# Attention in cycles of two pairs of heads, with their score blocks next to each other

## The chip, the cores and the metric

One core of one Trainium2 chip runs the kernel. The metric is the device time of one execution in microseconds (us). The core has five engines that each work through an instruction queue of their own: TensorE (PE, matrix products into the eight PSUM banks), VectorE (DVE), ScalarE (ACT), GpSimd (POOL) and SyncE (SP, which here issues nearly all DMA transfers).

## The reference

The input x has 32 sequences of 64 tokens of width 512. The context has the same shape. There are 32 heads of width 128.

```python
def reference(x, ctx, bias, mask, g_xattn, g_ffn, Wq, Wk, Wv, Wo, W, b, A, B, starts):
    q = layernorm(x) @ Wq                      # (32, 64, 32, 128)
    k, v = ctx @ Wk, ctx @ Wv
    score = einsum('bqhd,bkhd->bhqk', q, k) / sqrt(128) + bias
    probs = softmax(where(mask, score, -inf))  # masked entries are 0
    att = einsum('bhqk,bkhd->bqhd', probs, v) @ Wo
    x = x + tanh(g_xattn) * att
    n = layernorm(x)
    y = n @ W.T + b + where(use_lora, (n @ A.T) @ B.T, 0)   # adapter by sequence
    return x + tanh(g_ffn) * y
```

## The kernel before

The tokens are worked in two phases of 1,024 (`NPH`); a phase has eight tiles of 128 tokens (`NT`) and 16 pairs of heads (`NPR`). Nearly every large product is made of two parts per operand, a rounded high part and the rest, with three matmuls for each term (`mm3`). The projections q, k and v are also split into 2 x 2 blocks, and seven block products named p1 to p7 replace eight; `unit` computes them into the four banks px, py, pv and pz in the order p1, p6, p7, p5, p2, p4, p3, of which p2, p4 and p3 accumulate into px, pv and pz again, after these have been read once. ACT copies px into the destination, DVE adds the others to it. Each product is six matmuls of 128 x 128 weights by 512 columns.

A phase has three stages. `stage_a` computes all keys (stored to HBM as `kd`) and all values (`vd`). `run` is the attention: for each pair n of heads the q unit (42 matmuls into `qT`), `scores` (for each of two heads 16 products that fill halves of one bank, of 128 x 64 weights), the softmax, `pv` (probabilities by values into four banks, copied and split into `ch` and `cl`), and `oproj` (eight token tiles of six matmuls with the split output weights of the pair, added into `acc`). After the second phase's attention come the four chunks of the feed-forward part (`ffn_chunk`).

The order of work is written out by hand: every engine takes its instructions in the order in which the program issues them, and a matmul that needs a buffer waits for it there. Work off the matmuls is spread by generators that stand in the list `streams`. `beat()`, called after each product and each tile, takes one step of each of them, and `drain(g)` takes all that are left of one. Among them are `prep` (the blocks of the next q weights: seven casts on ACT, eleven operations on POOL), `prep_o` (the split of the output weights), `bias_mask` (mask added to the loaded bias, on POOL) and `softmax`. The scores of a head are worked on where they are issued:

```python
nc.vector.scalar_tensor_tensor(s, ps, SCALE, s, ALU.mult, ALU.add)     # L761, frees the bank
nc.vector.tensor_reduce(mx, s, AX.X, ALU.max)                          # L763
nc.gpsimd.tensor_tensor(s, s, mx.unsqueeze(2).to_broadcast([P, NT, S]), ALU.subtract)  # L764
nc.scalar.activation(s, s, AF.Exp)                                     # L765
beat()
```

The rest of the softmax goes by beats: sum, reciprocal, product with the row mask (L780 to L782, DVE), normalisation (L783, POOL), two 32 x 32 block transposes into `tp` (L775, DVE) and sixteen copies of a quarter into the block-diagonal tile `pt` (L792, ACT). Pair 0 of a phase has half of its copies done as transposes on DVE.

The cycle of pair n is: q unit up to p2, two oproj tiles of pair n - 2, the unit's p4 and p3, pv(n - 1), scores of n, six oproj tiles of pair n - 1. Scores are followed by oproj, but for pair 0, which has the next q unit behind it. PSUM tiles come from one pool of eight banks in turn. One buffer holds the pair's keys (`res[1]`, loaded after the scores of the pair before), two hold the values of two pairs, half of the tokens each (`res[2]`, `res[3]`), two hold `qT`, one `pt`, two the scores (`sm`), two `tp`.

Of the kernel before, what the change touches and what calls it, by code (L numbers as in the profile page):

```python
# [17 lines left out]
P = 128  # L18
# [3 lines left out]
S = 64  # L22
# [20 lines left out]
def flamingo_block(ctx: ExitStack, tc: tile.TileContext, x, ctxT, bias, mask, gx, gf,  # L43
# [24 lines left out]
    def drain(g):  # L68
        if g in streams:
            streams.remove(g)  # L70
            for _ in g:
                pass
# [625 lines left out]
    def attention(p, res, rest):  # L698
        b = {}

        def load_k(n):
            b["k", n] = big(res[1], [P, 2, TP], F32, f"kB{p}_{n}")
            nc.sync.dma_start(out=b["k", n], in_=kd[p][n])

        def load_v(q):
            b["v", q] = [big(res[2 + c], [P, 4, 512], F32, f"v{p}_{q}_{c}") for c in range(2)]
            for c in range(2):
                nc.sync.dma_start(out=b["v", q][c], in_=vd[p][q][:, c * 4:(c + 1) * 4, :])
# [5 lines left out]
        def bias_mask(n):  # L714
            yield
            yield
            for i in range(2):
                yield
                t = sm[n % 2][:, i]
                nc.gpsimd.tensor_tensor(t, t, masks[p][0], ALU.add)  # L720

# [5 lines left out]
        def enter():  # L727
# [10 lines left out]
            load_k(0)  # L738
            load_v(0)
# [28 lines left out]
        def softmax(n, pace):  # L768
            ss = [sm[n % 2][:, i] for i in range(2)]
            alone = pace is None  # L770
            tp = []

            def turn(i):
                tp.append(rows.tile([P, NT, S], F32, tag="row", name=f"tp{p}_{n}_{i}"))
                nc.vector.transpose(tp[i].rearrange("p a b -> p (a b)"), ss[i].rearrange("p a b -> p (a b)"))  # L775

            for i in range(2):
                nm = f"{p}_{n}_{i}"
                r = st.tile([P, NT], F32, tag="r", name=f"r{nm}")
                nc.vector.tensor_reduce(r, ss[i], AX.X, ALU.add)  # L780
                nc.vector.reciprocal(r, r)
                nc.vector.tensor_tensor(r, r, masks[p][1], ALU.mult)  # L782
                nc.gpsimd.tensor_tensor(ss[i], ss[i], r.unsqueeze(2).to_broadcast([P, NT, S]), ALU.mult)  # L783
                if alone and i:
                    turn(0)
                yield
            quads = [(h, qi, ki) for h in range(2) for qi in range(2) for ki in range(2)]

            def copy(f, i, of, h, qi, ki):
                src = slice(h * 64 + qi * 32, h * 64 + qi * 32 + 32)  # L790
                dst = slice(h * 64 + ki * 32, h * 64 + ki * 32 + 32)
                f(pt[dst, i, :, src], of[src, :, ki * 32:(ki + 1) * 32])  # L792

            if alone:
                for k, q in enumerate(quads):
# [361 lines left out]
```

## Time and profile before

| | us |
|---|---|
| median of 3 runs (1547.86 to 1548.68) | 1547.89 |
| the profiled execution | 1547.98 |
| its span, first to last instruction | 1545.8 |
| PE busy | 1538.4 |
| POOL busy | 1015.8 |
| DVE busy | 946.5 |
| ACT busy | 728.6 |

The granted TensorE clock is 1.000 over the span. The profile's page lists busy times, costliest groups by line and the chain of work that ended last; the chain of waits, the timeline and windows of it are answers from the same trace. The attention of the two phases runs from about 327 to 745 us and from 1060 to 1490 us. A busy PE is a modelled figure: records of matmuls overlap, and the starts of successive ones tell its pace. PE's L96 is the line of `mm3`, so its groups are told apart by tile (pa is oproj; px, py, pv, pz with q are the q unit; po is pv; ps is scores; ppk the plain key product). L87 and L88 are `split`, L293 and L297 the casts and differences of the weight blocks, L352, L357 and L374 the adds and copies of `unit`, L820 and L821 those of pv, L841 that of oproj.

### The profile page before, as it was taken

To read this page: it belongs to the slowest core of one execution; us is meant where nothing else is said; L and a number is where in the kernel's file an instruction comes from. 1 tells how busy PE (TensorE), PEld (TensorE's weight loads), DVE (VectorE), ACT (ScalarE), POOL (GpSimd) and SP (SyncE) were. 2 spreads that over 40 slices of the span, in tenths; PEclk is the share of its full clock that TensorE was granted. 3 is DMA by queue.
4 is the path that set the end of the run, shared out by engine and by line. 5 is a ranking of instruction groups with operands and counts; after the bars stand their busy time and mean duration, and the time that the engine had idled before them with its cause. 6 is when DMAs were issued, how large, how long until landed. Compare 5 with 4: busy or idle time off the path is not lost.

```text
span 1545.8 us, 24999 instructions
## 1 busy us (share of the span) xinstructions
PE 1538.4 (100%) x9080; PEld 1295.4 (84%) x9080; DVE 946.5 (61%) x1579; ACT 728.6 (47%) x1605; POOL 1015.8 (66%) x1128
## 2 busy tenths in 40 slices
PE   9999999999999999999999999999999999999999
PEld 7888888888888888888888888888888888888887
DVE  5675343377676757575686536437666676757763
ACT  6354233345555555556435423334555555555620
POOL 3898378967665757575589837896666665757410
PEclk9999999999999999999999999999999999999999
DMA  6654444374243424441565544438424342544201
GB/s 211 239 191 177 167 169 163 137 280 177 83 177 137 167 85 176 187 150 65 215 213 191 177 170 165 164 136 290 167 85 176 137 175 84 179 182 161 68 35 67
DMA packets 80989, 246.37 MB, mean 159 GB/s; under 512 B 9857, under 2 KB 10881, under 8 KB 72674
## 3 DMA queue, kind: packets, MB, share of 16 engines
q1 hardware_dynamic: 80578, 244.26, 43.9%
q8 instruction: 71, 1.16, 0.3%
q10 hardware_dynamic: 288, 0.52, 0.1%
q14 instruction: 52, 0.43, 0.1%
HBM read 171.35 MB, written 73.40 MB: 158 GB/s over the span
## 4 chain that ended last, share of the span: by engine, by line
PE 96%; DMA 2%; DVE 2%; issue 0%; ACT 0%; POOL 0%; SPq 0%; DVEq 0%; ACTq 0%; POOLq 0%
PE pa L96 22%; PE po L817 7%; PE pzv L96 6%; PE pvv L96 6%; PE pxv L96 6%; PE pzq L96 5%; PE pxq L96 5%; PE pxk L96 5%; PE pzk L96 5%; PE pvk L96 5%; PE pvq L96 5%; PE ps L759 4%; PE pf L96 4%; PE ppk L96 3%; PE pyv L96 3%; PE pyk L96 2%
## 5 line engine op out<-in xcount | busy, mean ns | idle before, releaser
L96 PE MATMUL pa<-wo,ch 128*128 128x512 f32 x1024 | 319.9, 393 | 0.0
L792 ACT COPY pt<-tp 32x256 f32<-32x256 f32 x496 | 200.3, 404 | 87.3 <-DVE tp L775 76.2
L88 POOL TENSOR_TENSOR wo<-rawo,wo 128x512 fp32r<-128x512 f32 x64 | 81.2, 1288 | 223.1 <-ACT wo L87 215.3
L96 PEld LDWEIGHTS pa<-wo,ch 128*128 128x128 f32 x1024 | 189.4, 188 | 40.0
L841 DVE TENSOR_TENSOR acc<-pa,acc 128x512 f32<-128x512 f32 x256 | 170.0, 673 | 79.5 <-PE pa L96 79.3
L96 PE MATMUL pa<-wo,cl 128*128 128x512 f32 x512 | 199.7, 390 | 0.0
L817 PEld LDWEIGHTS po<-pt,v 128*128 128x128 f32 x1024 | 119.1, 192 | 2.6 <-ACT pt L792 0.2
L821 DVE TENSOR_TENSOR cl<-po,ch 128x512 fp32r<-128x512 f32 x128 | 88.3, 691 | 51.9 <-ACT ch L820 51.4
L817 PE MATMUL po<-pt,v 128*128 128x128 f32 x1024 | 119.4, 275 | 0.0
L352 DVE TENSOR_TENSOR vt<-pvv,vt 128x512 f32<-128x512 f32 x64 | 44.1, 689 | 113.3 <-PE pvv L96 113.3
L96 PEld LDWEIGHTS pa<-wo,cl 128*128 128x128 f32 x512 | 96.1, 188 | 20.7
L820 ACT CAST ch<-po 128x512 fp32r<-128x512 f32 x128 | 75.0, 586 | 72.0 <-PE po L817 71.4
L765 ACT ACTIVATE sm<-sm 128x512 f32<-128x512 f32 x64 | 40.5, 633 | 122.7 <-POOL sm L764 122.7
L764 POOL TENSOR_TENSOR sm<-sm,mx 128x512 f32<-128x512 f32 x64 | 66.9, 1048 | 45.6 <-DVE mx L763 45.6
L374 ACT COPY vt<-pxv 128x512 f32<-128x512 f32 x32 | 18.8, 588 | 132.7 <-PE pxv L96 132.7
L352 DVE TENSOR_TENSOR kT<-pvk,kT 128x512 f32<-128x512 f32 x56 | 38.5, 688 | 69.4 <-PE pvk L96 68.8
L720 POOL TENSOR_TENSOR sm<-sm,madd 128x512 f32<-128x512 f32 x60 | 76.4, 1296 | 2.7 <-DMA sm<-bias 2.7
L783 POOL TENSOR_TENSOR sm<-sm,r 128x512 f32<-128x512 f32 x64 | 66.9, 1045 | 14.5 <-DVE r L782 11.1
L759 PE MATMUL ps<-kB,qT 128*64 128x64 f32 x2048 | 67.2, 224 | 0.3 <-DVE qT L352 0.3
L352 DVE TENSOR_TENSOR qT<-pzq,qT 128x512 f32<-128x512 f32 x64 | 44.2, 691 | 38.0 <-PE pzq L96 37.6
L352 DVE TENSOR_TENSOR vt<-pzv,vt 128x512 f32<-128x512 f32 x64 | 44.2, 691 | 37.1 <-PE pzv L96 36.9
L759 PEld LDWEIGHTS ps<-kB,qT 128*64 128x64 f32 x2048 | 62.5, 138 | 4.9 <-issue 0.7
(976 smaller groups left out, 3706.2 us busy)
## 6 DMA issues: line engine op xcount, KB each, us to landing
kd<-kT SPq DMA_DIRECT2D x64, 512.0 KB, 3.2
vd<-vt SPq DMA_DIRECT2D x128, 256.0 KB, 2.3
kB<-kd SPq DMA_DIRECT2D x32, 1024.0 KB, 4.9
v<-vd SPq DMA_DIRECT2D x32, 1024.0 KB, 8.7
rawq<-wq SPq DMA_DIRECT2D x32, 512.0 KB, 4.1
sm<-bias SPq DMA_DIRECT2D x64, 256.0 KB, 5.3
rawo<-wo SPq DMA_DIRECT2D x32, 512.0 KB, 3.5
rawk<-wk SPq DMA_DIRECT2D x31, 512.0 KB, 5.6
```

Source lines behind the costliest of these rows:

```text
L88: eng.tensor_tensor(lo, raw, hi.bitcast(F32), ALU.subtract)
L96: nc.tensor.matmul(ps, a, b, start=start and i == 0, stop=stop and i == 3 * n - 1, skip_group_check=True)
L352: nc.vector.tensor_tensor(o, ps, i, ALU.add)
L720: nc.gpsimd.tensor_tensor(t, t, masks[p][0], ALU.add)
L759: nc.tensor.matmul(ps[h * S:(h + 1) * S, t, :], qT[:, i, tok], kT[:, i, tok], start=True, stop=True)
L764: nc.gpsimd.tensor_tensor(s, s, mx.unsqueeze(2).to_broadcast([P, NT, S]), ALU.subtract)
L783: nc.gpsimd.tensor_tensor(ss[i], ss[i], r.unsqueeze(2).to_broadcast([P, NT, S]), ALU.mult)
L792: f(pt[dst, i, :, src], of[src, :, ki * 32:(ki + 1) * 32])
L817: nc.tensor.matmul(ps[:, t * P:(t + 1) * P], b["v", n // 2][c][:, t, hg * P:(hg + 1) * P], pt[:, i, c * 4 + t, :], start=True, stop=True)
L820: nc.scalar.copy(ch[:, i, sl], ps)
L821: nc.vector.tensor_tensor(cl[:, i, sl], ps, ch[:, i, sl].bitcast(F32), ALU.subtract)
L841: nc.vector.tensor_tensor(acc[t], ps, acc[t], ALU.add)
```

## The change

The loop over single pairs becomes a written order: q units 0, scores 0, q units 1 and 2, pv 0, scores 1 and 2 next to each other; then for each two pairs a and a + 1: q unit a, oproj(a - 3), pv(a - 2), q unit a + 1, oproj(a - 2), pv(a - 1), scores of a and a + 1. Pair 15 stands alone. A q unit is issued whole, and oproj tiles are issued eight at a time, except around the last pair, whose pv is issued in two halves between halves of oproj(14). Keys have two buffers (`res[1]`, `res[2]`); values are loaded for one pair (`res[3]`, eight runs of 256 elements a partition). The softmax generator is split in two: `normed` (sums and normalisation; the second pair of a cycle waits four beats first) and `turned` (transposes and the sixteen copies, now all on ACT for pair 0 as well). `turned` of a cycle's second pair is started at the end of the first one's pv. Bias and mask of pair n + 2 are issued from `turned(n)`. `prep_o(0)` starts before the scores of pair 0, the last pair's output weights get their own buffer, and what filled the time before the last pv (`fill`) moves ahead of oproj(14).

The diff:

```diff
--- before.py
+++ after.py
@@ -66,7 +66,7 @@
                 streams.remove(g)
     def drain(g):
-        if g in streams:
+        if g is not None and g in streams:
             streams.remove(g)
             for _ in g:
                 pass
@@ -699,25 +699,24 @@
         b = {}
         def load_k(n):
-            b["k", n] = big(res[1], [P, 2, TP], F32, f"kB{p}_{n}")
+            b["k", n] = big(res[1 + n % 2], [P, 2, TP], F32, f"kB{p}_{n}")
             nc.sync.dma_start(out=b["k", n], in_=kd[p][n])
-        def load_v(q):
-            b["v", q] = [big(res[2 + c], [P, 4, 512], F32, f"v{p}_{q}_{c}") for c in range(2)]
-            for c in range(2):
-                nc.sync.dma_start(out=b["v", q][c], in_=vd[p][q][:, c * 4:(c + 1) * 4, :])
+        def load_v(n):
+            b["v", n] = big(res[3], [P, NT, 256], F32, f"v{p}_{n}")
+            nc.sync.dma_start(out=b["v", n], in_=vd[p][n // 2][:, :, n % 2 * 256:(n % 2 + 1) * 256])
         def load_bias(n):
             for i in range(2):
                 nc.sync.dma_start(out=sm[n % 2][:, i].rearrange("p a b -> p (a b)"), in_=bias[p, 2 * n + i])
         def bias_mask(n):
-            yield
-            yield
+            for _ in range(4):
+                yield
             for i in range(2):
-                yield
                 t = sm[n % 2][:, i]
                 nc.gpsimd.tensor_tensor(t, t, masks[p][0], ALU.add)
+                yield
         def bias_add(i):
             t = sm[0][:, i]
@@ -736,6 +735,8 @@
                 return
             fetch("q", p * NPR + 1, "r0")
             load_k(0)
+            load_bias(1)
+            load_k(1)
             load_v(0)
         def enter_late():
@@ -765,65 +766,67 @@
             nc.scalar.activation(s, s, AF.Exp)
             beat()
...
+        def normed(n, wait):
+            for _ in range(wait):
+                yield
             for i in range(2):
-                nm = f"{p}_{n}_{i}"
-                r = st.tile([P, NT], F32, tag="r", name=f"r{nm}")
-                nc.vector.tensor_reduce(r, ss[i], AX.X, ALU.add)
+                t = sm[n % 2][:, i]
+                r = st.tile([P, NT], F32, tag="r", name=f"r{p}_{n}_{i}")
+                nc.vector.tensor_reduce(r, t, AX.X, ALU.add)
                 nc.vector.reciprocal(r, r)
                 nc.vector.tensor_tensor(r, r, masks[p][1], ALU.mult)
...
+                nc.gpsimd.tensor_tensor(t, t, r.unsqueeze(2).to_broadcast([P, NT, S]), ALU.mult)
+                yield
+        def turned(n, pace=(1, 2, 2, 3, 2, 2, 2, 2)):
+            tp = []
             for i in range(2):
-                turn(i)
-                yield
-            todo = [(i, q) for i in range(2) for q in quads]
+                tp.append(rows.tile([P, NT, S], F32, tag="row", name=f"tp{p}_{n}_{i}"))
+                nc.vector.transpose(tp[i].rearrange("p a b -> p (a b)"), sm[n % 2][:, i].rearrange("p a b -> p (a b)"))
+                yield
+            if n + 2 < NPR:
+                load_bias(n + 2)
+                b["m", n + 2] = bias_mask(n + 2)
+                streams.append(b["m", n + 2])
+            todo = [(i, h, qi, ki) for i in range(2) for h in range(2) for qi in range(2) for ki in range(2)]
             for k in pace:
-                for i, q in todo[:k]:
-                    copy(nc.scalar.copy, i, tp[i], *q)
+                for i, h, qi, ki in todo[:k]:
+                    src = slice(h * 64 + qi * 32, h * 64 + qi * 32 + 32)
+                    dst = slice(h * 64 + ki * 32, h * 64 + ki * 32 + 32)
+                    nc.scalar.copy(pt[dst, i, :, src], tp[i][src, :, ki * 32:(ki + 1) * 32])
                 del todo[:k]
                 yield
...
+        def both(*gs):
+            for g in gs:
+                yield from g
+        def pv(n, cs=(0, 1)):
+            drain(b["s", n])
+            for c in cs:
+                for i in range(2):
+                    ps = psum(f"po{p}_{n}_{i}_{c}")
+                    for t in range(4):
+                        nc.tensor.matmul(ps[:, t * P:(t + 1) * P], b["v", n][:, c * 4 + t, i * P:(i + 1) * P],
+                                         pt[:, i, c * 4 + t, :], start=True, stop=True)
+                    sl = slice(c * 512, (c + 1) * 512)
+                    nc.scalar.copy(ch[:, i, sl], ps)
+                    nc.vector.tensor_tensor(cl[:, i, sl], ps, ch[:, i, sl].bitcast(F32), ALU.subtract)
+                    beat()
+            if cs[-1] == 1 and n + 1 < NPR:
+                load_v(n + 1)
+                if ("n", n + 1) in b:
+                    drain(b["n", n + 1])
+                    b["s", n + 1] = turned(n + 1)
+                    next(b["s", n + 1])
+                    next(b["s", n + 1])
+                    streams.append(b["s", n + 1])
         def prep_o(n):
             raw = raw_of.pop(("o", p * NPR + n))
-            t = big(res[4], [P, 2, 1024], F32R, f"wo{p}_{n}")
+            t = big(res[4] if n < NPR - 1 else res[1], [P, 2, 1024], F32R, f"wo{p}_{n}")
             b["o", n] = t
             for i in range(2):
                 sl = slice(i * 512, (i + 1) * 512)
@@ -832,84 +835,109 @@
             if n + 1 < NPR:
                 fetch("o", p * NPR + n + 1, "r1")
-        def oproj(n, t):
+        def oproj(n, ts=range(NT), beside=None):
+            drain(ob.get(n))
             w = b["o", n]
...
+            for t in ts:
+                ps = psum(f"pa{p}_{n}_{t}")
+                sl = slice(t * P, (t + 1) * P)
+                mm3(ps, [((ch[:, i, sl], cl[:, i, sl]),
+                          (w[:, 0, i * 512:(i + 1) * 512], w[:, 1, i * 512:(i + 1) * 512])) for i in range(2)])
+                nc.vector.tensor_tensor(acc[t], ps, acc[t], ALU.add)
+                if n == NPR - 1 and p < NPH - 1:
+                    nc.sync.dma_start(out=x1d[t * P:(t + 1) * P, :], in_=acc[t])
+                beat()
+                if beside:
+                    beside(t)
+            if ts[-1] == NT - 1 and n + 1 < NPR - 1:
+                start_o(n + 1)
+        ob, qT = {}, {}
+        def start_o(n):
+            ob[n] = prep_o(n)
+            streams.append(ob[n])
+        def run(xq, prefetch, before_last, last_unit, fill, last, between=None):
+            qb = {}
+            def start_q(n, *a):
+                qb[n] = prep("q", p * NPR + n, *a)
+                streams.append(qb[n])
+            def q_unit(n):
                 g = p * NPR + n
-                qT = kqp.tile([P, 2, TP], F32, tag="kq", name=f"qT{g}")
+                drain(qb.get(n))
                 if n == 0:
-                    qb = prep("q", g + 1, nc.vector, 2)
-                    streams.append(qb)
+                    start_q(1, nc.vector, 2)
+                elif n + 1 < NPR:
+                    fetch("q", g + 1, "r0")
+                    if n == 1:
+                        start_q(2, nc.gpsimd, 3)
                 else:
-                    streams.append(bias_mask(n))
-                end = unit(wt[("q", g)], xq, None, k_dst(qT), f"q{g}", tuple(carry))
+                    before_last()
+                qT[n] = kqp.tile([P, 2, TP], F32, tag="kq", name=f"qT{g}")
+                end = unit(wt[("q", g)], xq, None, k_dst(qT[n]), f"q{g}", tuple(carry))
                 carry.clear()
+                end()
+                if 1 < n < NPR - 1:
+                    start_q(n + 1, nc.gpsimd)
                 if n == NPR - 1:
                     last_unit()
...
+            def score(*ns):
+                for n in ns:
+                    drain(b.get(("m", n)))
+                for n in ns:
+                    for i in range(2):
+                        scores(n, i, qT[n], b["k", n])
+                for n in ns:
                     if n + 2 < NPR:
-                        fetch("q", g + 2, "r0")
-                    elif n + 2 == NPR:
-                        before_last()
-                if n == NPR - 5:
+                        load_k(n + 2)
+                for k, n in enumerate(ns):
+                    b["n", n] = normed(n, 4 * k)
+                    if k or n == NPR - 1:
+                        streams.append(b["n", n])
+                    else:
+                        b["s", n] = both(b.pop(("n", n)), turned(n))
+                        streams.append(b["s", n])
+            b["m", 1] = bias_mask(1)
+            streams.append(b["m", 1])
+            q_unit(0)
+            enter_late()
+            start_o(0)
+            score(0)
+            q_unit(1)
+            q_unit(2)
+            pv(0)
+            score(1, 2)
+            for a in range(3, NPR - 1, 2):
+                q_unit(a)
+                oproj(a - 3)
+                pv(a - 2)
+                q_unit(a + 1)
+                oproj(a - 2)
+                pv(a - 1)
+                score(a, a + 1)
+                if a == NPR - 5:
                     prefetch()
...
+            n = NPR - 1
+            q_unit(n)
+            oproj(n - 3)
+            pv(n - 2)
+            score(n)
+            oproj(n - 2, beside=between)
+            pv(n - 1)
+            fill()
+            drain(ob[n - 1])
+            start_o(n)
+            oproj(n - 1, range(4))
+            pv(n, (0,))
+            oproj(n - 1, range(4, NT))
+            pv(n, (1,))
+            last(lambda t: oproj(n, range(t, t + 1)), acc)
         return enter, run
@@ -919,7 +947,7 @@
     def frow(nm):
         rk[0] += 1
-        return rwp.tile([P, 512], F32, tag=f"r{1 + rk[0] % 3}", name=nm)
+        return rwp.tile([P, 512], F32, tag=("r0", "r2", "r3")[rk[0] % 3], name=nm)
     def x1_row(c, t):
         return acc1[(c % NCH) * 4 + t] if c // NCH == NPH - 1 else x1t[c][:, t, :]
@@ -1049,22 +1077,23 @@
                 streams.append(fb)
-            def last(finish, attend, o, acc):
-                nonlocal more, kt0
+            def fill():
+                nonlocal kt0
                 g = (p + 1) * NPR
-                finish()
-                fetch("k", g + 1, "r1")
                 kt0 = k_tile(g)
                 while (2, 1) not in first[1]:
                     next(fb)
                 plain_half(wt["k", g], first[1], k_dst(kt0), f"k{g}", 0)
-                attend()
+            def last(o, acc):
+                nonlocal more
+                fetch("k", (p + 1) * NPR + 1, "r1")
                 gate.append(True)
                 for t in range(NT):
                     o(t)
                 drain(fb)
                 more = acc_stats(p, acc)
-            run(xq, prefetch, before_last, last_unit, last)
+            run(xq, prefetch, before_last, last_unit, fill, last)
         else:
             weights = ffn_weights(qt)
@@ -1077,7 +1106,11 @@
                 if t == 2:
                     ffn_norm(1, 0)
-            def last(finish, attend, o, acc):
+            def fill():
+                drain(weights)
+                ffn_chunk(0, first=False)
+            def last(o, acc):
                 acc1.extend(acc)
                 def moments(t):
@@ -1096,10 +1129,6 @@
                     if t == 3:
                         ffn_norm(3, 0)
-                finish()
-                drain(weights)
-                ffn_chunk(0, first=False)
-                attend()
                 for t in range(NT):
                     o(t)
                     if t < 4:
@@ -1109,7 +1138,7 @@
                 ffn_chunk(1, rest_of)
                 ffn_chunk(2, first=False)
                 ffn_chunk(3)
-            run(xq, ffn_fetch, ffn_rows, last_unit, last, between)
+            run(xq, ffn_fetch, ffn_rows, last_unit, fill, last, between)
         res, rot = qt, res + rest
```

## The prediction

> **What bounds the kernel now.** I read the page first, then the chain of work that ended last, then the timeline of one attention cycle and of the first q unit of a phase, and last the waits of PE. The page, span and busy times:
>
> ```profile
> span 1545.8 us, 24999 instructions
> PE 1538.4 (100%) x9080; PEld 1295.4 (84%) x9080; DVE 946.5 (61%) x1579; ACT 728.6 (47%) x1605; POOL 1015.8 (66%) x1128
> ```
>
> TensorE leaves almost no gap. The chain (start, us, what) gives the length of one pair's cycle:
>
> ```profile
> 554.46 2.02 PE ps L759 x64
> 556.47 8.41 PE pa L96 x36
> ...
> 577.12 3.57 PE po L817 x32
> 580.69 2.02 PE ps L759 x64
> ```
>
> A cycle is 580.69 - 554.46 = 26.23 us: 42 matmuls of the q unit and 48 of oproj, 32 records of pv, 64 of scores. In stage A, the chain has a unit of 42 in 9.52 us (33.89 to 43.41), so 0.2267 each. The timeline has 64 score records in 2.09 and 48 in 1.62, so 0.0294 each, 1.88 a block. The work alone is 90 x 0.2267 + 3.57 + 1.88 = 25.85; **0.38 us a cycle are lost around the score block**, where PE changes to 128 x 64 tiles and back (36 pa take 8.41, not 8.16, after it). [...]
>
> The timeline (start, us, engine, line) of what follows a score block today:
>
> ```profile
> 580.62 2.09 PE L759 MATMUL ps<-kB,qT 128*64 128x64 f32 x64
> 582.01 0.68 DVE L761 SCALAR_TENSOR_TENSOR sm<-ps,sm 128x512 f32<-128x512 f32 x1
> 582.72 0.69 DVE L763 TENSOR_REDUCE mx<-sm 128x8 f32<-128x512 f32 x1
> 583.33 0.68 DVE L761 SCALAR_TENSOR_TENSOR sm<-ps,sm 128x512 f32<-128x512 f32 x1
> 583.49 1.04 POOL L764 TENSOR_TENSOR sm<-sm,mx 128x512 f32<-128x512 f32 x1 [0.83 <-DVE mx L763]
> ```
>
> Per head DVE needs 1.32 us (582.01 to 583.33), PE 0.94. The surplus is hidden: oproj comes next and asks little of DVE. Once a phase no oproj follows, after pair 0, and there PE does stop:
>
> ```profile
> 329.77 1.66 PE L96 MATMUL pxq<-x0p,wq1p 128*128 128x512 f32 x6
> ...
> 333.18 0.63 ACT L765 ACTIVATE sm<-sm 128x512 f32<-128x512 f32 x1 [0.91 <-POOL sm L764]
> ...
> 333.72 0.57 ACT L357 COPY qT<-pxq 128x512 f32<-128x512 f32 x1
> ...
> 334.32 0.69 DVE L352 TENSOR_TENSOR qT<-pyq,qT 128x512 f32<-128x512 f32 x1 [0.89 <-ACT qT L357]
> 334.93 0.68 DVE L780 TENSOR_REDUCE r<-sm 128x8 f32<-128x512 f32 x1
> ...
> 336.59 0.65 DVE L352 TENSOR_TENSOR qT<-pvq,qT 128x512 f32<-128x512 f32 x1
> ...
> 337.30 1.65 PE L96 MATMUL pvq<-x0p,wq1p 128*128 128x512 f32 x6 [0.42 <-DVE qT L352]
> ```
>
> The unit's first copy stands behind the second head's exponential on ACT, the adds into qT stand behind it and the softmax sums on DVE, and product p4 waits until the add has read bank pv. p4 was due 30 matmuls after 329.77 plus 0.1 of restart, at 336.7; it came 0.6 late, and p3 (339.37) again 0.6. With 0.1 to restart each, 1.4 us. PE's waits name no others inside attention:
>
> ```profile
> PE pzq L96 <- DVE qT L352: 0.8, 2, 0.4
> PE pvq L96 <- DVE qT L352: 0.8, 2, 0.4
> ```
>
> **The change, part by part.** *Fewer score blocks*: 16 a phase become 9 (0; seven of two pairs; 15). Each of 14 joins removes 0.38: **-5.3 us**.
>
> *A q unit right after four score heads* (7 a phase). The old order had oproj behind the scores and two oproj tiles between p2 and p4; both covers go. From the first score matmul (0): the first DVE operation starts at 1.39 as now (pv before it is unchanged); the fourth maximum starts at 1.39 + 3 x 1.32 + 0.71 = 6.06, ends 6.75; POOL's subtraction (0.08 later, 1.04) ends 7.87; the exponential starts 7.90, the unit's copy 0.54 later, 8.44; the py add 0.60 later, 9.04. Behind that the change puts the second head's sum, reciprocal and product (0.61 + 0.71 + 0.24 + 0.30 = 1.86 to the next add, from rows of both timelines): pv add 10.90, and p4 0.75 later, 11.65. The unit starts at 2.02 + 1.88 = 3.90 and p4 is due 6.91 after it, 10.81. So PE waits 0.84, and 0.1 to restart: 0.95. p3 then comes at 13.1; its bank is read by 12.84, so it doesn't wait. [...] There are 12 (all but the first of each phase), their drains are in the -5.3; the wait is 12 x 0.95 = **+11.4**. Bounds: 0.3 if the chain is one step shorter, 1.4 as after pair 0; I take 0.95, since every step has a row.
>
> One reading is open in these rows: the chain ends a DMA (acc<-x) at 333.31, so that DMA, not the exponential, might have held the copy. But the copy starts 0.54 us behind the exponential, and 0.54 is also the step from an exponential (559.65) to the cast behind it (560.19) in the steady cycle, so I take it as queued behind. [...] If the DMA were the cause, the +11.4 would fall to about 0.
>
> *First join of each phase* (pairs 1, 2). wq3's preparation starts with pv(0), so four of its steps stand in the score beats; POOL's steps (0.73) fall between the subtractions. The fourth ends at 9.25, not 7.87; the copy ends at 10.4 against p2 due at 9.45 (wait 1.1 with restart), p4 13.06 against 11.9 (1.25). 2.35 each, **+4.7**. Bounds 0.95 and 3.5.
>
> *Start of a phase.* wo0's split moves into score(0): a cast on ACT (0.57) and 1.28 on POOL between the two subtractions, twice. Second subtraction ends 335.1, exponential 335.15, second cast, copy 336.17 to 336.75. p2, due 335.3, comes 1.5 late, p4 (add 338.6 to 339.3) 1.1 late; p3 is in time, since pair 0's eight DVE transposes go to ACT. With restarts 2.75. The second unit follows at once, 342.2: behind both normalisations (339.7) POOL has seven steps of wq2 to p6's weights, 7 x 0.73 = 5.1, 344.8; p6 is due at 343.6: 1.35. Sum 4.1 against 1.4 now: **+2.7 a phase, +5.4**. Bounds -1.4 (all waits gone) and +5.
>
> *At nothing.* Values by pairs: 1 MB in 1 KB runs; today's 1 MB takes 8.7 us from issue; even doubled it fits in the 20.4 us of a unit and oproj between two pv; beyond that it would cost its overrun. SP's queue: load_v waits for pv, two load_k for the scores, the bias for the transposes (13.5 after the scores' start); behind them are the next rawq and the mask. Bias lands at about 19 (5.3), the masks and wq's 8 us on POOL end at about 28.4, before the next unit at 29. At phase starts the DMA engines are full from 312 to 336 us; bias(1) and kB(1) now come earlier, half the values less; acc's landing moves by about 1 us and nothing waits for it. pv's sixteen copies to pt still have a unit and oproj. Ends: fill and half of oproj(14) (10.9 us) cover pair 15's transposes and copies (about 7.5); ffn_chunk's stall (0.4 at 1459.5) may go. Taken as 0.
>
> Sum: -5.3 + 11.4 + 4.7 + 5.4 = **+16.2 us**. Profiled execution 1547.98 (span 1545.8 and 2.2 around it), median 1547.89, 0.1 apart: **1564**.
>
> **Rivals.** (1) *The gain is kept: faster.* DVE gets from the scores to the pv add sooner, say because the second head's sums fit into the 1 us in which it waits for the copy; this decides from a chain 0.5 us shorter than worked out, where the wait falls below the 0.38 saved. Against it: five of the rows that make it up stand in the timeline above. Then -5.3 and at the starts -2.8 to 0: 1540 to 1545. (2) *POOL sets the pace in every join*, as in the first: 2.35 in 14 joins, +32.9 - 5.3 + 5.4 = +33, 1581. For it: POOL has the most work beside PE (66%), and the half cycle behind a join carries 21.6 of 29 us (eight softmax operations of 1.05, masks 2.6, wq 8.0, wo 2.6); against it: wq's preparation should be over before pv. [...] That two pairs don't stand together at all is excluded by the order written out.
>
> **How the numbers follow.** Forecast 0.56, its own range 1554 to 1574 (0.5 to 1.4 a join, the starts' bounds in part); (1) 0.17; (2) 0.17; (3) 0.10. From 1543, in the middle of (1), to 1582, in the middle of (2), some 0.2 is left out. A measurement here can tell 0.2%, 3 us, from no change: faster 0.17, same 0.10, slower 0.73.
>
> **What would show it.** Score blocks of 128 records, about 3.9 us, 9 a phase; PE waits on DVE qT at product p4 once per join, 14 times, near 0.6 to 1 us each, with the copy L357 directly behind an exponential; a two-pair cycle of 53.0 us where two now take 52.46; wq2's p6 waiting on POOL. Wrong: a two-pair cycle of 52.1, no pvq waits; or waits at p2.

## The result, and the profile after

The changed kernel takes 1568.18 us (median of four runs, 1567.4 to 1569.6); the kernel before, beside it on the same chip, 1548.0. The ratio is 1.0131, with a 95% interval of 1.0119 to 1.0143: slower, by 20.2 us, where 16.2 were forecast. The profiled execution took 1567.4 us with a span of 1565.6, 19.8 more than before, and it is this difference that is accounted for below.

The page of the kernel after, its span, the engines' busy times and the chain that ended last by engine:

```profile
span 1565.6 us, 25205 instructions
...
PE 1540.2 (98%) x9080; PEld 1291.5 (82%) x9080; DVE 945.5 (60%) x1565; ACT 739.0 (47%) x1621; POOL 1017.4 (65%) x1128
...
PE 84%; POOL 4%; DVE 3%; issue 3%; DMA 3%; ACT 2%; DVEq 0%; SPq 0%; POOLq 0%
```

TensorE has the same 9080 matmuls, but 2% of the span is now without one, and the chain runs through it for 84% only; before it was 96%. The other engines did hardly more than before (POOL 1017.4 against 1015.8, ACT 739.0 against 728.6), so nobody became the bound by the amount of its work. The waits of PE (total, number, longest):

```profile
PE pvq L96 <- DVE qT L352: 9.8, 16, 0.9
PE pxq L96 <- ACT qT L357: 3.7, 4, 1.4
PE po L812 <- ACT pt L798: 2.4, 3, 1.0
PE pzq L96 <- DVE qT L352: 2.2, 2, 1.1
```

Two waits of 0.7 for wq2 on POOL come behind these. Sixteen waits at p4 are the fourteen joins and the second unit of each phase. The chain shows the joined block and the length of a two-pair cycle:

```profile
517.70 3.91 PE ps L760 x128
529.20 1.66 PE pvq L96 x6
532.21 10.88 PE pa L96 x48
...
567.08 3.57 PE po L812 x32
570.65 3.91 PE ps L760 x128
```

570.65 - 517.70 is 52.95 us; two of the old cycles took 2 x 26.23 = 52.46. The 128 score matmuls run in one block of 3.91, oproj takes 10.88 for 48 matmuls, which is 0.2267 each and leaves no loss, and p4 (pvq) heads its own piece since PE had to wait for it. The timeline of the join that starts at 411.74 shows on what:

```profile
417.31 1.04 POOL L765 TENSOR_TENSOR sm<-sm,mx 128x512 f32<-128x512 f32 x1 [0.34 <-DVE mx L764]
417.94 0.69 DVE L764 TENSOR_REDUCE mx<-sm 128x8 f32<-128x512 f32 x1
...
418.70 1.04 POOL L765 TENSOR_TENSOR sm<-sm,mx 128x512 f32<-128x512 f32 x1 [0.34 <-DVE mx L764]
...
419.78 0.63 ACT L766 ACTIVATE sm<-sm 128x512 f32<-128x512 f32 x1 [0.76 <-POOL sm L765]
...
420.32 0.57 ACT L357 COPY qT<-pxq 128x512 f32<-128x512 f32 x1
420.92 0.69 DVE L352 TENSOR_TENSOR qT<-pyq,qT 128x512 f32<-128x512 f32 x1 [1.15 <-ACT qT L357]
...
421.22 1.52 PE L96 MATMUL pxq<-x0p,wq5p 128*128 128x512 f32 x6
421.53 0.67 DVE L776 TENSOR_REDUCE r<-sm 128x8 f32<-128x512 f32 x1
...
422.56 0.68 DVE L352 TENSOR_TENSOR qT<-pvq,qT 128x512 f32<-128x512 f32 x1
...
423.30 1.42 PE L96 MATMUL pvq<-x0p,wq5p 128*128 128x512 f32 x5 [0.56 <-DVE qT L352]
```

This is the chain of the prediction link by link: fourth maximum, subtraction, exponential, the unit's copy 0.54 behind it, the py add, the second head's sum, reciprocal and product, the pv add, p4. Counted from the first score matmul the pv add starts at 10.82 (worked out: 10.90) and p4 at 11.56 (11.65). The copy's product, the first pxq, ran from 415.62 to 417.28, and ACT was idle for 0.76 us ahead of the exponential at 419.78: the copy stood in ACT's order, not in want of ACT.

How late p4 is can be read from the last PE rows: p2's six matmuls start at 421.22 and take 6 x 0.2267 = 1.36, so p4 was due at 422.58 and came 0.72 late. The 0.56 in brackets counts from the modelled end of the last matmul, which is later. The waits of the changed kernel that are summed up further down are counted from the starts in this way; those in lists and brackets are the profile's.

### The profile page after: what moved, and what is told of

Same layout as the page of the kernel before. It is cut to its first block, busy times and chain, and to the rows that moved or that the text cites. A ratio compares the mean times of both kernels' runs of the same rounds, so it can differ in the third digit from the quotient of the medians.

```text
span 1565.6 us, 25205 instructions
## 1 busy us (share of the span) xinstructions
PE 1540.2 (98%) x9080; PEld 1291.5 (82%) x9080; DVE 945.5 (60%) x1565; ACT 739.0 (47%) x1621; POOL 1017.4 (65%) x1128
## 4 chain that ended last, share of the span: by engine, by line
PE 84%; POOL 4%; DVE 3%; issue 3%; DMA 3%; ACT 2%; DVEq 0%; SPq 0%; POOLq 0%
PE pa L96 21%; PE po L812 7%; PE pxv L96 6%; PE pzv L96 5%; PE pvv L96 5%; PE pxk L96 5%; PE pzk L96 5%; PE pvk L96 5%; PE pf L96 4%; PE pvq L96 3%; PE ps L760 3%; PE pzq L96 3%; PE ppk L96 3%; PE pyv L96 3%; PE pyk L96 2%
## 5 line engine op out<-in xcount | busy, mean ns | idle before, releaser
L96 PE MATMUL pa<-wo,ch 128*128 128x512 f32 x1024 | 316.3, 390 | 0.0
L846 DVE TENSOR_TENSOR acc<-pa,acc 128x512 f32<-128x512 f32 x256 | 176.2, 690 | 138.7 <-PE pa L96 138.5
L798 ACT COPY pt<-tp 32x256 f32<-32x256 f32 x512 | 206.7, 404 | 24.5 <-DVE tp L787 12.5
L816 DVE TENSOR_TENSOR cl<-po,ch 128x512 fp32r<-128x512 f32 x128 | 87.5, 691 | 52.2 <-ACT ch L815 52.1
L352 DVE TENSOR_TENSOR qT<-pvq,qT 128x512 f32<-128x512 f32 x64 | 44.0, 687 | 35.8 <-PE pvq L96 35.6
L190 POOL TENSOR_TENSOR vs<-wvr,wvr 128x512 f32<-128x512 f32 x24 | 30.8, 1292 | 51.8 <-DMA wvr<-wv 51.7
```

The source lines that it names most:

```text
L96: nc.tensor.matmul(ps, a, b, start=start and i == 0, stop=stop and i == 3 * n - 1, skip_group_check=True)
L352: nc.vector.tensor_tensor(o, ps, i, ALU.add)
L798: nc.scalar.copy(pt[dst, i, :, src], tp[i][src, :, ki * 32:(ki + 1) * 32])
L816: nc.vector.tensor_tensor(cl[:, i, sl], ps, ch[:, i, sl].bitcast(F32), ALU.subtract)
L846: nc.vector.tensor_tensor(acc[t], ps, acc[t], ALU.add)
```

## The experiments

All times are medians beside runs of the kernel before on the same chip; a cycle is the time from the start of one joined score block to the next.

**1. The second head's normalisation later.** If the softmax sums between the two adds make p4 late, two beats more for them should take the wait away.

```
-        def normed(n, wait):
+        def normed(n, wait, gap=0):
...
-                yield
+                for _ in range(1 if i else 1 + gap):
+                    yield
...
-                    b["n", n] = normed(n, 4 * k)
+                    b["n", n] = normed(n, 4 * k, 2 if len(ns) > 1 and k == 0 else 0)
```

> The changed kernel with one edit: in a join of two pairs the first pair's second-head sum, reciprocal and product (and its normalisation) go two beats later, behind the unit's pv and pz adds. Theory (the prediction's chain: these three stand between the py add and the pv add that p4 waits for): the p4 wait, 0.72 plus 0.11 of restart in the profile of the changed kernel, goes in 12 joins (-10.0 us) and the 0.87 + 0.11 at p4 of the first join of each phase nearly so (-1.5): about 1556.5 us, 1555 to 1559; two-pair cycle 52.1 instead of 52.95. Rival A (the copy behind the four exponentials is late enough alone, or POOL sets the pace): no change, 1568, p4 waits stay above 0.5. Rival B (the sums only move the wait from p4 to p3): p3 waits of 0.4 or more in each join, 1562 to 1566.

Measured: 1567.72 us (ratio 1.0125, 1.0109 to 1.0140). The waits at p4 go in the joins, and the cycles are 52.11. Yet the total hardly moves, because one cycle in each phase, the one after the prefetch for the next stage, grows to 55.91 and 58.98:

```profile
PE po L813 <- ACT pt L799: 8.1, 4, 3.7
```

The two cycles differ though their waits are alike (start, us, what):

```profile
648.83 2.94 PE L813 MATMUL po<-pt,v 128*128 128x128 f32 x24 [3.54 <-ACT pt L799]
```

```profile
1388.42 5.49 PE L813 MATMUL po<-pt,v 128*128 128x128 f32 x24 [3.69 <-ACT pt L799]
```

In the second phase the same 24 matmuls behind the wait take 5.49 us instead of 2.94: the granted clock is 0.50 from 1389 to 1393, where in the first phase it stays 1.00. The cause of the waits at p4 is confirmed, the expected total missed by 11 us; what took the gain is the subject of 5 and 6.

**2. One more change of tile size, in the kernel before.** The last quarter of pv is put between the two heads' scores, so PE goes to 128 x 64 tiles and back once more in each of 30 pairs, with the same matmuls.

```
+                    pv(n - 1, slice(0, 3))
...
                     scores(n, i, qT, b["k", n])
+                    if n and i == 0:
+                        pv(n - 1, slice(3, 4))
```

> The kernel before with one edit: the last of pv's four tiles goes between the two heads' scores of pairs 1 to 15, so that TensorE changes to 128 x 64 tiles and back once more in each pair; no work is added. Theory (0.32 to 0.38 us are lost per change and return): 30 more changes, +9.6 to +11.4 us, 1557.5 to 1559.5. Rival (the 0.38 belongs to the first matmuls of oproj behind the scores or to the amount of score work, not to the change of tiles): within 2 us of 1548.

Measured: 1559.62 us (1.0076, 1.0061 to 1.0091), 11.6 more, 0.1 above the range. Not all of it is the change of tiles. The cycles grow from 26.23 to 26.55, which is 0.32 us for one change and return and 9.6 for thirty; most of the rest is a wait in the feed-forward part that is not among PE's waits in the kernel before:

```profile
PE pt L991 <- DVE fa L983: 1.8, 1, 1.8
```

So a loss of 0.32 comes with each change into the small tiles and back, with the same matmuls; it is most of the 0.38 that the prediction found lost around a score block.

**3. wo0's split behind the second q unit.**

```
             enter_late()
-            start_o(0)
             score(0)
             q_unit(1)
+            start_o(0)
             q_unit(2)
```

> The changed kernel with one edit: the split of pair 0's output weights starts behind q unit 1 instead of before the scores of pair 0. Theory (its casts and its work on POOL stand between the two subtractions and hold the copy): p2's wait of 1.51 + 0.11 in unit 1 goes, p4's falls from 1.02 to about 0.3, wq2's p6 wait of 0.85 stays or falls: -2.4 to -3.3 a phase, 1561.5 to 1563.5. Rival (the transfers of the phase's start hold the copy, or wq2's preparation simply waits longer): 1567 to 1569.

Measured: 1566.32 us (1.0114, 1.0097 to 1.0130); missed. The unit's p2 no longer waits, as expected, but from the first scores to the next it is 31.34 us in the first phase and 28.19 in the second, where the changed kernel has 29.04 and 29.05. SP's queue and POOL in the first phase:

```profile
332.47 0.33 SPq L262 DMA_DIRECT2D rawq<-wq  x1
...
341.30 0.73 POOL L286 TENSOR_TENSOR wsq<-rawq 128x256 f32<-128x256 f32 x1 [2.55 <-DMA rawq<-wq]
```

The raw weights of wq2 were issued at 332.47, behind acc and pair 2's keys, and POOL waited 2.55 us for them. That the order of SP's queue costs nothing at a phase's start was wrong. Unit 2 waits for wq2's blocks in both phases (0.43, 1.19 and 0.68 us in the first, 1.10 and 1.11 in the second), but in the first the granted clock drops behind these waits (stretch, PE, PEld, DVE, ACT, POOL busy, granted clock, DMA share and rate), and most of the 3.15 us between the phases is this:

```profile
344.00:348.00 4.00, 3.32 (x10) 2.18 (x9) 0.00 (x0) 3.87 (x11) 4.00 (x7) 0.57 0.00 2
348.00:352.00 4.00, 4.00 (x11) 3.10 (x11) 1.38 (x2) 3.50 (x8) 4.00 (x5) 0.57 0.42 131
```

**4. Pair 1's mask later.** In the changed kernel q unit 0 waits at p3 (the pzq row above), which the prediction didn't have. Its timeline in the changed kernel:

```profile
323.31 2.91 POOL L718 TENSOR_TENSOR sm<-sm,madd 128x512 f32<-128x512 f32 x2
...
323.55 0.68 DVE L352 TENSOR_TENSOR qT<-pvq,qT 128x512 f32<-128x512 f32 x1
324.15 0.91 DVE L286 TENSOR_TENSOR wsq<-rawq 128x256 f32<-128x256 f32 x1
...
324.99 1.51 DVE L297 TENSOR_TENSOR wq1p<-wsq,wq1p 128x256 fp32r<-128x256 f32 x1
...
326.42 0.68 DVE L352 TENSOR_TENSOR qT<-pzq,qT 128x512 f32<-128x512 f32 x1
...
327.25 1.63 PE L96 MATMUL pzq<-x0p,wq0p 128*128 128x512 f32 x6 [1.07 <-DVE qT L352]
```

Two steps of wq1's preparation on DVE take 0.91 and 1.51 beside pair 1's mask on POOL; the pz add stands behind them. In the kernel before, POOL is idle there, and the same steps take 0.41:

```profile
324.05 0.41 DVE L286 TENSOR_TENSOR wsq<-rawq 128x256 f32<-128x256 f32 x1
324.38 0.41 DVE L297 TENSOR_TENSOR wq1p<-wsq,wq1p 128x256 fp32r<-128x256 f32 x1
```

The edit gives the mask to unit 2:

```
-            b["m", 1] = bias_mask(1)
-            streams.append(b["m", 1])
             q_unit(0)
...
             q_unit(1)
+            b["m", 1] = bias_mask(1)
+            streams.append(b["m", 1])
             q_unit(2)
```

> The changed kernel with one edit: adding the mask to pair 1's bias on POOL goes from q unit 0 to q unit 2. In q unit 0 of the changed kernel p3 waits 1.23 us for DVE, which the prediction did not have. Theory (VectorE's 128 x 256 operations of wq1 take 0.73 to 0.91 us while POOL works and 0.41 while it is idle; POOL now works there): the operations after 324 us take 0.41 again, the wait goes with its 0.08 of restart, -2.6 us, about 1565.5. Rival (the operations are late for their casts on ACT or for their raw weights): wait stays, 1567 to 1569.

Measured: 1568.3 us (1.0128, 1.0113 to 1.0143). The wait of unit 0 is gone (the first scores start at 327.14 instead of 328.80, and both steps take 0.41 again), but the mask now meets wq2's preparation on POOL and the next scores come 30.27 us after the first instead of 29.04; the prefetch's cycle was longer too, 56.87 instead of 54.17 (a wait of 2.00 us at pv(11), and behind it a granted clock of 0.57 from 652 to 656). The cause of unit 0's wait is confirmed, the gain in the total is not.

**5. The prefetch two units later.** In the changed kernel:

```profile
627.89 10.98 SPq L410 DMA_DIRECT2D c<-ctxT  x8
...
639.22 0.33 SPq L262 DMA_DIRECT2D rawq<-wq  x1
...
645.17 0.41 ACT L293 CAST wq14p<-rawq 128x256 fp32r<-128x256 f32 x1 [6.03 <-DMA rawq<-wq]
```

SP issues the next stage's eight transfers for 11 us, wq14's raw weights are behind them, and ACT's cast of wq14 waits 6.03 us with pair 11's copies to pt queued behind it; pv(11) is late, and the cycle takes 54.17.

```
                 q_unit(a + 1)
+                if a == NPR - 3:
+                    prefetch()
...
-                if a == NPR - 5:
-                    prefetch()
```

> The changed kernel with one edit: the 2 MB that are loaded ahead for the next stage are issued after q unit 14 instead of after the scores of pairs 11 and 12. There pv(11) waits 1.1 to 1.2 us for the copies to pt, which the prediction did not have. Theory (the loads stand on SP's queue ahead of the raw weights of q 14; the cast of these holds ACT's queue and the copies behind it): the two-pair cycle of that place falls from 54.2 to 52.95 in both phases, -2.5 us, 1565.7. Rival (POOL or DVE is late there for another reason): cycle stays at 54, 1568.

Measured: 1564.83 us (1.0108, 1.0092 to 1.0124); the cycles there are 52.94 like the others. Confirmed.

**6. Edits 1 and 5 together.**

> Both edits: the second head's sums two beats later, and the loads for the next stage after q unit 14. The first edit alone brought the cycles to 52.11 but made the cycle with the loads 55.9 and 59.0. Theory (the edit gives its 0.84 a join everywhere once the loads are out of the way of the copies to pt): every two-pair cycle 52.1, first joins 53.05, 1553 to 1555 us, still above 1548 by the starts of the phases (about +7). Rival (putting the sums off makes pv wait by itself): 1560 or more.

Measured: 1553.93 us (median of five, 1.0043, 1.0030 to 1.0056). The first join's cycles are 53.08 and 53.05, the steady ones 52.1, and 52.29 in the prefetch's place of the first phase; one in the second phase is 53.54, where the chain runs through the transfer of wq22's raw weights for 12.36 us and pv(3) waits 1.15 for the copies behind their cast (the profiled execution took 1556.72). The total is as expected; the gain that edit 1 had lost was lost at the prefetch. There edit 1 had made things worse: with later sums the transposes come later, and thirteen of the sixteen copies to pt stood behind the late cast instead of eight.

**7. The starts too.** On top of 6: wo0's and acc's loads behind unit 1, wo0's split behind unit 2, the mask as in 4, pair 2's keys loaded behind unit 1, wq2's preparation begun three beats earlier, wq3's in unit 2, the sums of pair 0 later as well, and at a phase's end the last wo's split behind half of oproj(14).

> The edits of the run before, and the start of a phase cleared: pair 0's output weights are split from pv(0) on, the mask of pair 1 is added in q unit 2, the transfers of acc and of keys 2 are issued behind those of the raw weights of q 2, the preparation of q 2 starts three beats earlier, that of q 3 within q unit 2; at the end the last output weights are split after the first half of oproj(14). Theory (the starts cost 4.6 + 2.6 by POOL's, ACT's and the transfers' order, the first joins 0.8 each by POOL): scores 0 to scores 1 in 26.7 to 28 us instead of 29.05, first join 52.1 to 52.4, 1543 to 1548 us, so faster than both kernels or even with the first. Rival (wq2 cannot be ready earlier, since its raw weights wait for the buffer of wq1): the starts keep 2 us each, 1548 to 1551.

Measured: 1561.96 us (1.0092, 1.0078 to 1.0106); missed by 14 us and more. The waits of units 0 to 2 are gone but for one of 0.5, and a larger one has come in each phase, 7.5 at most:

```profile
PE po L815 <- ACT pt L801: 16.7, 4, 7.5
```

```profile
342.01 6.15 SPq L752 DMA_DIRECT2D acc<-x  x8
348.57 0.33 SPq L262 DMA_DIRECT2D rawq<-wq  x1
```

wq3's raw weights are behind acc on SP's queue, and the cast of wq3 now stands ahead of pair 0's copies on ACT: the same pattern as in 3 and 5.

**8. The unit's first copy on DVE.** Edit only on the changed kernel, and only in units behind a join: the copy goes to DVE, so it no longer stands behind the exponential.

```
-        nc.scalar.copy(u, px)
+        (first or nc.scalar.copy)(u, px)
...
+                           nc.vector.tensor_copy if n > 2 and n % 2 else None)
```

> The changed kernel with one edit: in the q units that follow a join, the first copy out of px goes from ACT, where it stands behind the fourth exponential, to DVE, where it stands behind the fourth maximum. Theory (the exponential in front of the copy on ACT is one of the two things that make p4 late, the second head's sums the other): copy ends 7.4 us after the first score instead of 9.0, but the sums that filled DVE's idle time now come behind it; pv add done at 11.0, p4's wait falls from 0.72 to 0.2 to 0.35, -0.4 to -0.5 in 14 joins and p2's wait of 0.68 in the first joins goes: 1560 to 1563. Rival (DVE's own queue is the bound and the copy's place on ACT does not matter): 0.69 more work on DVE makes p4 wait 1.2 or more, 1575.

Measured: 1560.58 us (1.0083, 1.0069 to 1.0097), as expected, and the cycles are 52.27. One place in ACT's order is worth most of the wait: the copy behind the exponential, and not a DMA, was what the adds waited for.

**9. The starts in order.** As 7, but wo0's raw weights where they were, acc behind unit 2 and so behind wq3's raw weights on SP's queue, and wq3's preparation where it was.

> As the run with the starts cleared, but the transfers of acc go behind those of the raw weights of q 3, the raw output weights of pair 0 are fetched early as in the changed kernel, and q 3 is prepared from pv(0) on. There units 1 and 2 had no wait, and pv(0) waited 7.5 us since the cast of wq3 on ACT waited for raw weights that landed behind acc. Theory (without that wait scores 0 to scores 1 take 25.3 to 26 us, scores 0 come 1.3 us earlier, first joins 53.0, all other cycles 52.1): 1542 to 1545 us, faster than the kernel before by 0.2 to 0.35%. Rival (pv(0) now waits for the copies because POOL and ACT have q 2 and the softmax at once): some 2 us more each phase, 1546 to 1549.

Measured: 1552.29 us (1.0025, 1.0014 to 1.0035); missed. The starts are good now (25.24 and 25.28 us from the first scores to the next), but the first joins take 57.40 and 57.36: wo0's split and wq3's preparation now stand on POOL ahead of the four subtractions and between them, and p2 waits for the unit's copy.

```profile
PE pxq L96 <- ACT qT L357: 6.6, 2, 3.3
```

The windows of these microseconds (columns as in 3) show a second loss:

```profile
360.00:364.00 4.00, 2.33 (x11) 1.57 (x9) 3.51 (x6) 2.15 (x6) 4.00 (x6) 1.00 1.05 377
364.00:368.00 4.00, 2.38 (x7) 1.95 (x8) 3.33 (x5) 1.16 (x3) 2.17 (x3) 0.80 0.98 409
368.00:372.00 4.00, 4.00 (x15) 3.12 (x15) 3.86 (x10) 2.60 (x7) 2.09 (x2) 0.77 0.38 132
```

Behind a wait of 3.3 us the granted clock is 0.80 and 0.77 in the two windows from 364 to 372.

**10. Cover put back.** The changed kernel with edit 5, and with half of an output projection, four tiles, between the joined scores and the q unit (the old order had six there).

```
             for a in range(3, NPR - 1, 2):
+                oproj(a - 3, range(4))
                 q_unit(a)
-                oproj(a - 3)
+                oproj(a - 3, range(4, NT))
```

> The changed kernel with the loads for the next stage after q unit 14, and one more edit: four of the eight oproj tiles of pair a - 3 go between the joined scores and the q unit, four behind it; the sums stay where they are. Theory (the wait at p4 comes because no oproj stands behind the four heads any more; 5.4 us of it, 24 matmuls, give DVE, POOL and ACT the time): no wait at p4 or p2 in any join, all two-pair cycles 52.1, the starts as in the changed kernel: 1551 to 1553.5. Rival (the cover only moves the wait to the next unit's weights, whose preparation has 9 us left for POOL's 8, or to the copies before pv): cycles of 52.6 or more, 1558 or more.

Measured: 1554.48 us (1.0041, 1.0025 to 1.0056), a microsecond above the range. The cycles are 52.09 and the first ones 52.36 and 52.39 with no edit to the softmax order at all. What the expectation lacked is in the last stage: PE waits 1.87 us for DVE's work on fa, an operand of the feed-forward part, which it doesn't in the changed kernel, with a granted clock of 0.65 and 0.93 in the windows of 4 us from 1448 on:

```profile
PE pa L96 <- DVE fa L1011: 1.9, 1, 1.9
```

The joins ask for work behind them that leaves DVE, ACT and POOL time; the old order had it.

**11. Cover and starts together**: 10, with the starts of 9, wo0's split begun with unit 2, and the later sums for pair 0 alone.

> The run with the starts in order, with the oproj cover behind every join in place of the later sums, and the output weights of pair 0 split from q unit 2 on. There the first join of each phase took 57.4 us: p2 waited 3.46 for the copy, because wq3's preparation stood between the subtractions on POOL, and the clock fell to 0.8 behind it. Theory (the cover hides that wait): first joins 52.1 to 53, all cycles 52.1, starts 25.2: 1541 to 1544, faster than the kernel before by 0.25 to 0.45%. Rival (POOL's backlog at the first join is longer than 5.4 us of cover, or oproj of pair 0 now waits for its weights or for acc): first joins 54 or more, 1545 to 1549.

Measured: 1545.31 us (11 runs, 1544.34 to 1546.44) beside 1547.99 of the kernel before: ratio 0.9983 (0.9974 to 0.9991). That is faster than both kernels, by 22.9 us and by 2.7; the interval against the kernel before lies below 1, though the gain is less than the 0.2% set as the bound in the prediction. The expected 1541 to 1544 is missed by 1.3 us: the cycles are 52.09 and the starts 25.45 as expected, the first joins 53.20 a little more, and the wait for fa in the last stage was not in the expectation. What PE still waits for:

```profile
PE pa L96 <- DVE fa L1016: 1.9, 1, 1.9
PE pvq L96 <- DVE qT L352: 1.5, 2, 0.8
```

**12. The last p4 waits.** On top of 11, edit 1 for the first join of a phase alone.

> The fast version (covered joins and starts in order) with one more edit: in the first join of a phase, too, the second head's softmax step of pair 1 stands two beats later. There no output projection covers the join; its p4 waits of 0.88 and 0.99 are put down to that step standing between two adds on DVE. My theory: these two waits go and the first cycle falls from 53.20 to about 52.3, which is 1.7 to 1.9 less in all: 1543.4 to 1544 us, 0.26 to 0.29% below the kernel before. Rival: POOL, which still prepares wq3 between the subtractions there, sets the pace: the step held back is then late for its own readers, the transposes, and the wait turns up at p2 or at pv: 1545 us or above.

Measured: 1545.36 us (0.9983, 0.9973 to 0.9992): no change in the median; missed. In the second phase the first cycle falls as expected, from 53.20 to 52.56; in the first it is 53.31, and p4 still waits 0.92 there. The expectation was wrong in its premise too: four tiles of oproj(0) do cover this join. With pair 1's step held back, other sums and a transpose stand between the adds, and the pv add starts at 369.18 where 11 has it at 369.24. The two versions agree at 2.6 to 2.7 us below the kernel before.

## Why the prediction was right, and where it was off

**The loss around a score block.** Taken at 0.38, measured by the cycles of 2 at 0.32, and by joined cycles without a wait at 52.46 - 52.11 = 0.35 (6) and 52.46 - 52.09 = 0.37 (10, 11) a join. The prediction's sum calls this loss a drain; no run shows what TensorE does in it, only that this time goes with each change to the 128 x 64 tiles and back. Fourteen joins are then worth 4.5 to 5.2; predicted 5.3, and 4.9 is used below. That rival (1) did not come is no fault of this term: the changed kernel saves it too, and pays more than that in waits.

**The wait at p4**, the step that decided: right in each link of the timeline above. It was 0.72 in the steady joins with 0.11 to restart, against 0.84 and 0.1; 12 x 0.83 is 10.0 instead of 11.4. The chain came out 0.09 shorter than worked out (p4 at 11.56 instead of 11.65), which is the size of the error. That the copy stood behind the exponential, the one reading left open, is settled by 8. Rival (2) failed because wq's preparation was indeed over before the joins, except in the first of each phase; rival (3), which had the 0.10 for no change, by half a microsecond a join, since the wait and its restart cost 0.83 and the loss that a join saves is 0.35 to 0.37. "Waits at p2", which the prediction gave as a sign of being wrong, came only where its own sum had such waits, in the first joins and in unit 1.

**The first joins.** Waits at p2 (0.68) and p4 (0.87), as named, with 0.11 each 1.77 a join instead of 2.35: 3.5 instead of 4.7. The mechanism, wq3's steps between the subtractions, is in the timeline; its size was over-estimated.

**The starts.** Unit 1's p2 waits 1.51 and p4 1.02 (named 1.5 and 1.1); unit 2's wait for wq2 0.85 instead of 1.35. With restarts 3.7 a phase, net of today's 1.4 this is 4.6 for both, against 5.4.

**At nothing: the step that failed.** Three things in it were not nothing. First, pair 1's mask now runs beside wq1's preparation in unit 0, and p3 waits 1.23 and 0.08 to restart in each phase, 2.6 together; the prediction put the mask at a free place on POOL and didn't ask what DVE did beside it. Second, the prefetch delays the next raw weights: two cycles of 54.17 and 54.26, 2.5 together; the prediction listed SP's queue for a usual cycle and left out the one with the prefetch in it. Third, at the ends pv(15) waits behind wo's casts (0.58 and 0.18), where 0.41 of a stall in the last stage went: about +0.55. And "nothing waits for" acc's landing was wrong as a general statement: in 3 POOL waited 2.55 us for weights behind acc, in 7 pv(0) up to 7.5 for copies behind the cast of such weights.

**The sum of what was measured**: -4.9 + 10.0 + 3.5 + 4.6 + 2.6 + 2.5 + 0.55 = 18.9 of the 19.8. About 0.3 more is in the last store; the remaining 0.6 isn't placed. The forecast of 16.2 is 3.6 below the 19.8, from errors of both signs: the waits it named were 3.4 smaller (18.1 instead of 21.5), what it had at nothing was 5.7, and with the 0.4 on the score blocks and the last microsecond that makes the difference. That errors of both signs left the sum this near is luck in part.

**What stays open.** The prefetch's cycle varied between kernels (54.17 in the changed one, 56.87 in 4, 55.91 and 58.98 in 1). That it is the prefetch is shown by 5 and 6, and the traces show what the differences are made of: in 4 pv(11) waits 2.00 us instead of 0.94 and the clock drops to 0.57 behind the wait, in 1 more copies stand behind the cast (thirteen instead of eight), and in its second phase the clock drops too (0.50). Why the wait was longer in 4, and what decides whether the clock drops, was not tried. Nor was it settled why the edit of 12 shortens the first join of the second phase and not that of the first.

## What to carry to other kernels

Joining blocks of small tiles does save the loss around each block, 0.32 to 0.37 us each here, but it also joins their evacuation: cost the chain behind the doubled block up to the first instruction that needs a bank back, engine by engine in queue order, and leave a stretch of work behind the block that asks little of the other engines. Costing the steady cycle is not enough: list the queues (SP's too) for the cycles that hold something rare, a prefetch or a phase's start. In 5 the cast that waited 6.03 us for a late weight held pair 11's copies, queued behind it on ACT. Where an edit's wait goes and the total stays, look for the next queue; here a gain over the kernel before came only when the prefetch, the cover and the starts were right at once.

## What the runs showed of the hardware

The DVE steps of wq1's preparation that met pair 1's mask on POOL, both operands in SBUF, didn't slow down in proportion, they ended about 0.3 us after a POOL instruction did. In the rows of experiment 4 POOL's pair of masks ends at 323.31 + 2.91 = 326.22 and the DVE step of 1.51 at 324.99 + 1.51 = 326.50, 0.28 later; the step that lasts 0.91 ends at 325.06, and the second mask starts at 324.74, so the first had ended some 0.3 before. With POOL idle the same steps take 0.41. The add at 323.55, in the midst of the first mask, takes one operand from PSUM and isn't lengthened (0.68). Beside the mask the two steps cost DVE 0.50 and 1.10 us more; the prediction costed the mask on POOL alone.

Some waits of PE cost more than themselves, because the granted clock was lower behind them: 0.57 in the next 4 us behind a wait of 2.00 (experiment 4), 0.80 and 0.77 behind one of 3.3 (experiment 9), 0.50 behind one of 3.69 (experiment 1, second phase). The length of one wait doesn't settle it. Behind 3.54 us in the first phase of experiment 1 the clock stayed 1.00, behind 0.43 and 1.19 close together in experiment 3 it was 0.57 for 8 us, and the waits of up to 1.4 us in the changed kernel left its mean at 1.000. What does settle it no run here tried.
